# Counting edges with one-hot products: two columns of edges per product, one-hot values in runs of four

## The chip, the cores and the metric

The kernel runs on one core of one Trainium2 chip. The core has five engines that work side by side, each through its own queue: TensorE (PE: matrix products, and PEld: the loading of their weights), VectorE (DVE), ScalarE (ACT), GpSimd (POOL) and SyncE (SP, which starts transfers). The metric is the device time of one execution in microseconds (us), the median of several runs.

## The reference

The kernel is a four-layer network on 4608 tokens of 256 channels (two images of 48 x 48). The part that matters here is the graph attention inside layer 2. There are 1,048,576 edges, drawn for 65,536 nodes, while the graph has only T = 4608. An index that is too large reads the last node, and a target that is too large is dropped. So most of the valid edges have the last node as their source. Cut to what matters:

```python
M = Bc * Nc                                   # 4608 nodes
h = (x_flat @ W_gat).reshape(M, HEADS, NUM_EXPERTS)
e = leaky_relu(a_src[src] + a_dst[dst], negative_slope=0.2)
ee = jnp.exp(e - e_max[dst])
denom = jax.ops.segment_sum(ee, dst, num_segments=M)
msg = h[src] * (ee / (denom[dst] + 1e-16))[:, :, None]
agg = jax.ops.segment_sum(msg, dst, num_segments=M)
```

All edges from the last node to one target give the same term. The kernel therefore needs only a count for each of the 4608 targets, and treats the few other edges one by one.

## The kernel before

`Edges.sort_list` packs each edge into a key (a flag, the source counted down from the last node, 13 bits of target), and keeps the 64 largest keys of each of 16 lists in each of the 128 partitions: `slots`, 1024 keys a partition. In a key of the last node's edges the bits above the target hold the flag alone. `sort_rest` collects 16 columns of other keys into `oth` (16 x 4 = 64 columns are set aside), and the rest goes to DRAM.

`count_last` makes the count. The target is split into `lo` (its low 7 bits, 128 values) and `hi` (36 values). Of the 1024 columns of `slots` it takes 16 at a time, 64 groups in all. For each group VectorE writes two bf16 one-hot tiles: `ol` (L1322, 128 partitions x 16 columns x 128 values) and `oh` (L1326, 36 values x 16 columns). For each column TensorE multiplies them (L1328: `ol[:, j, :]` as weights, `oh[:, :, j]` as the moving operand of 36 columns), and all 1024 products add into one PSUM tile `cp`, 128 x 36. At the end one copy (L1333) moves `cp` to `cnt`. Both one-hot tiles have two buffers, so VectorE is at most two groups ahead of TensorE.

`count_last` is a generator that yields after each group. Its caller, `behind_gathers` in `graph_scores`, runs some steps of another piece of work after each: `pieces(AHEAD, BESIDE)`, the dense expert products for four stretches of 384 tokens. Each expert has seven steps of products (L1769, 192 moving columns, f32) with a VectorE or ScalarE operation behind each (L1778 to L1793, L1775, L1784), and 12 chains of second-layer products (L1810, 256 columns).

While this runs, GpSimd issues 128 indirect transfers (`gs`, L1427, and `gd`, L1431), one of each for each of 64 columns of other edges. They fetch rows of the node tables for `add_edges`. Later `add_edges` takes them in eight sets of eight columns (`GQ = 8`): a first sum `e<-gs,gd` (L1445) needs all 16 transfers of its set. Exponentials on ScalarE (L1448) follow, then for each column a one-hot row (`ol`, L1457), a wide product tile (`wide`, L1459, four buffers), and two products into `fp` (L1463, 360 columns). The sum at L1613 ends this stage, and the rest of the graph scores follow.

The order of the instructions in each engine's queue is not the order of the source. A scheduler sets it when the program is built, from its own estimates of durations, and each queue is then a fixed list. In the built program before, the first `e<-gs,gd` stands in VectorE's queue behind the last of the 64 groups.

Of the kernel before, what the change touches and what calls it, by code (L numbers as in the profile page):

```python
# [18 lines left out]
F32 = mybir.dt.float32  # L19
I32 = mybir.dt.int32  # L20
BF16 = mybir.dt.bfloat16
AF = mybir.ActivationFunctionType
ALU = mybir.AluOpType
# [4 lines left out]
P = 128  # L28
NB, C, HH, WW = 2, 256, 48, 48
L = HH * WW  # L30
T = NB * L
NT = T // P
# [66 lines left out]
def bc(ap, shape, axis):  # L99

    return ap.unsqueeze(axis).to_broadcast(shape)
# [1096 lines left out]
class Edges:  # L1198
# [93 lines left out]
    def count_last(self, E):  # L1292


        nc, tc = E.nc, E.tc
        n, LO = self.NL * self.SLOT, P
        GC = n // self.GROUPS
        HI = T // LO
        with (
            tc.tile_pool(name="gcnt", bufs=1) as wp,  # L1300
            tc.tile_pool(name="gcntps", bufs=1, space=PSUM) as ps,
        ):
            field = wp.tile([P, n], I32, name="field")
            ids_i = field[:, : HI * GC].rearrange("p (h g) -> p h g", h=HI)
            nc.gpsimd.iota(ids_i, pattern=[[1, HI], [0, GC]], base=0, channel_multiplier=0)
            ids = wp.tile([P, HI, GC], BF16, name="ids")
            nc.vector.tensor_copy(ids, ids_i)
            lo_ids = wp.tile([P, LO], BF16, name="lo_ids")
            nc.vector.tensor_copy(lo_ids, self.iota)
            bits = self.slots.bitcast(I32).rearrange("p l s -> p (l s)")  # L1310
            lo = wp.tile([P, n], BF16, name="lo")
            hi = wp.tile([P, n], BF16, name="hi")
            nc.vector.tensor_single_scalar(field, bits, LO - 1, ALU.bitwise_and)
            nc.vector.tensor_copy(lo, field)

            nc.vector.tensor_single_scalar(field, bits, 7, ALU.logical_shift_right)
            nc.vector.tensor_scalar(hi, field, float(-(self.FLAG >> 7)), None, ALU.add)
            cp = ps.tile([LO, HI], F32, name="cp")
            for g in range(n // GC):
                gs = slice(g * GC, (g + 1) * GC)  # L1320
                ol = wp.tile([P, GC, LO], BF16, tag="ol16", name="ol16", bufs=2)
                nc.vector.tensor_tensor(  # L1322
                    ol, bc(lo[:, gs], [P, GC, LO], 2), bc(lo_ids, [P, GC, LO], 1), ALU.is_equal
                )
                oh = wp.tile([P, HI, GC], BF16, tag="oh16", name="oh16", bufs=2)
                nc.vector.tensor_tensor(oh, bc(hi[:, gs], [P, HI, GC], 1), ids, ALU.is_equal)  # L1326
                for j in range(GC):
                    nc.tensor.matmul(  # L1328
                        cp, lhsT=ol[:, j, :], rhs=oh[:, :, j],
                        start=g == 0 and j == 0, stop=g == n // GC - 1 and j == GC - 1,  # L1330
                    )
                yield
            nc.vector.tensor_copy(self.cnt, cp)  # L1333


def target_maxima(E, edges, t_src, taken, best):
# [1502 lines left out]
```

## Time and profile before

| what | value |
|---|---|
| median of 3 runs (lowest to highest) | 4859.35 us (4858.32 to 4860.77) |
| profiled execution: its own time, its span | 4857.55 us, 4855.5 us |
| PE, DVE, ACT, POOL busy over the span | 4419.2, 3404.9, 2613.8, 2595.7 us |
| mean granted TensorE clock | 0.963 |
| the 64 groups: first `ol` to the copy of `cp` | 3373.05 to 3612.04 us |
| the 128 transfers: first start to last end | 3372.61 to 3639.77 us |
| products of `add_edges`: first start to the sum at L1613 | 3615.88 to 3695.88 us |

The profile is of one execution. Each row gives a start in us from the span's start and a length, with the engine, the line, and what was written from what. Rows that follow one another on an engine and are alike are merged, with their number (x16). What stands in brackets is the idle time of the engine before it and what ended it. TensorE's products overlap, so a length is a latency, and what a product costs in a stream is the distance between starts. An f32 product stands in the profile as two records.

### The profile page before, as it was taken

The page shows a single profiled execution, that of the slowest core. Times are in us where ns is not written, and L with a number is a line of the kernel's source. Part 1 is how long each engine was busy: PE and PEld are TensorE (multiplying, and loading weights), DVE is VectorE, ACT ScalarE, POOL GpSimd, SP SyncE. Part 2 cuts the span into 40 slices and gives each one's busy share as a digit, 9 for nine tenths or more (in the row PEclk, how much of TensorE's full clock was granted, in tenths as well). Part 3 has the DMA queues.
Part 4 walks back from the last instruction along what each step waited for, and adds up shares of the span by engine and source line. Part 5 has one row for each costly group of instructions (what it writes and reads, how often), then busy time and mean ns, then how long its engine had stood idle before and what let it go on. Part 6 is the DMA issues. An engine that isn't in the chain of part 4 may idle for free. (4 is left out here: it accounts for less than half of the span.)

```text
span 4855.5 us, 65017 instructions
## 1 busy us (share of the span) xinstructions
PE 4419.2 (91%) x23472; PEld 3283.1 (68%) x23472; DVE 3404.9 (70%) x5615; ACT 2613.8 (54%) x4390; POOL 2595.7 (53%) x2037
## 2 busy tenths in 40 slices
PE   7899999999999999988999999978998879999987
PEld 4666666667766667765555555547976558989855
DVE  4788888888888778887999924464887514453533
ACT  6888987888788888884223222323222423333311
POOL 3799887778888889887000000001880634445422
PEclk8999999999999999999999999999999889999988
DMA  3222222232221212223110000001111530000045
GB/s 98 71 87 86 79 92 80 87 99 90 76 83 56 73 63 82 86 75 124 47 39 31 33 5 13 1 35 34 33 27 55 159 106 24 14 11 7 11 142 161
DMA packets 160991, 312.47 MB, mean 64 GB/s; under 512 B 30855, under 2 KB 115055, under 8 KB 158084
## 3 DMA queue, kind: packets, MB, share of 16 engines
q1 hardware_dynamic: 144596, 271.49, 16.8%
q0 software_dynamic: 12304, 22.91, 2.1%
q10 hardware_dynamic: 3744, 13.66, 1.0%
q8 instruction: 192, 3.15, 0.3%
q14 instruction: 155, 1.27, 0.1%
HBM read 227.68 MB, written 80.31 MB: 63 GB/s over the span
## 5 line engine op out<-in xcount | busy, mean ns | idle before, releaser
L808 POOL TENSOR_TENSOR hcp<-ho,cc 128x768 f32<-128x768 f32 x768 | 1426.6, 1868 | 271.5 <-DVE ho L803 120.7
L672 PE MATMUL db<-ident,dbt 128*128 128x128 f32 x4608 | 791.1, 279 | 86.1 <-DVE ho L801 29.1
L672 PEld LDWEIGHTS db<-ident,dbt 128*128 128x128 f32 x4608 | 564.5, 142 | 408.9 <-issue 151.2
L698 PE MATMUL y<-ident,hcp 128*128 128x128 f32 x4608 | 742.7, 276 | 20.6 <-POOL hcp L808 20.5
L803 DVE TENSOR_TENSOR_SCAN ho<-he,state,db 128x384 f32<-128x384 f32 x640 | 627.6, 1005 | 123.2 <-PE db L672 85.7
L801 DVE TENSOR_TENSOR_SCAN ho<-he,state,db 128x384 f32<-128x384 f32 x640 | 622.6, 1002 | 121.6 <-PE db L672 95.2
L698 PEld LDWEIGHTS y<-ident,hcp 128*128 128x128 f32 x4608 | 557.8, 143 | 50.4 <-POOL hcp L808 26.9
L655 POOL TENSOR_SCALAR dbt<-dtt,bt 128x512 f32<-128x512 f32 x576 | 458.8, 806 | 118.1 <-ACT dtt L448 73.9
L662 ACT ACTIVATE he<-dt,negab 128x384 f32<-128x384 f32 x768 | 445.0, 609 | 128.1 <-DVE ho L803 124.7
L662 ACT ACTIVATE he<-dt,negaf 128x384 f32<-128x384 f32 x768 | 448.0, 611 | 107.4 <-DVE ho L801 100.5
L653 ACT ACTIVATE dbt<-dtt,bt 128x512 f32<-128x512 f32 x576 | 407.0, 712 | 4.3 <-PE db L672 3.9
L382 PE MATMUL mm<-xw,w_cv 128*128 128x384 f32 x768 | 316.1, 498 | 32.0 <-ACT xs L392 28.5
L1288 POOL PARTITION_ALL_REDUCE most<-most x1 | 0.4, 420 | 619.3 <-DVE most L1287 619.3
L1019 PE MATMUL pf<-t,wfc 128*128 128x384 f32 x768 | 254.9, 487 | 2.6 <-ACT hid L1023 2.2
L1038 PE MATMUL po<-hid,wfc 128*128 128x384 f32 x768 | 253.6, 486 | 0.0
L1023 ACT ACTIVATE hid<-pf,vec 128x384 f32<-128x384 f32 x192 | 109.7, 580 | 212.6 <-PE pf L1019 212.2
L1019 PEld LDWEIGHTS pf<-t,wfc 128*128 128x128 f32 x768 | 145.6, 190 | 106.0 <-ACT hid L1023 4.1
L1038 PEld LDWEIGHTS po<-hid,wfc 128*128 128x128 f32 x768 | 146.2, 190 | 101.5
L139 POOL TENSOR_TENSOR tv<-at 128x384 f32<-128x384 f32 x54 | 53.8, 997 | 253.1 <-ACT at L2507 121.0
L1810 PE MATMUL po<-w,hid 128*128 128x256 f32 x672 | 169.8, 382 | 0.0
L1191 POOL TENSOR_TENSOR xres<-xres,y 128x384 f32<-128x384 f32 x24 | 24.1, 1005 | 259.7 <-DVE y L1187 259.7
L382 PEld LDWEIGHTS mm<-xw,w_cv 128*128 128x128 f32 x768 | 118.9, 193 | 51.9 <-ACT xs L392 39.4
(659 smaller groups left out, 9115.5 us busy)
## 6 DMA issues: line engine op xcount, KB each, us to landing
cc<-bcd SPq DMA_DIRECT2D x96, 768.0 KB
xw<-xi_d SPq DMA_DIRECT2D x24, 774.0 KB
y_d<-y SPq DMA_DIRECT2D x28, 384.0 KB
down<-in_m_down SPq DMA_DIRECT2D x9, 1152.0 KB
up<-in_m_up SPq DMA_DIRECT2D x9, 1028.0 KB
xi_d<-xz SPq DMA_DIRECT2D x48, 192.0 KB
z_d<-xz SPq DMA_DIRECT2D x36, 256.0 KB
y<-z_d SPq DMA_DIRECT2D x12, 768.0 KB
```

The source lines that it names most:

```text
L382: nc.tensor.matmul(px, lhsT=w_cv[b, s][:, d * 4 + k, :], rhs=xw[:, d, o : o + W], start=k == 0, stop=k == 3,)
L653: nc.scalar.activation(to, at, AF.Copy, scale=b_n)
L655: nc.gpsimd.tensor_scalar(to, at, b_n, 1.0, ALU.mult, ALU.mult)
L662: nc.scalar.activation(hes[k], pc["dt"][:, d, :], AF.Exp, scale=nega[pc["s"]][:, d * NS + n : d * NS + n + 1])
L672: nc.tensor.transpose(dbs[k][:, j * P : (j + 1) * P], dbt[k // DB][:, j, d * P : (d + 1) * P], E.ident)
L698: nc.tensor.matmul(pc["yt"][j][:, d * P : (d + 1) * P], lhsT=hc[:, j * P : (j + 1) * P], rhs=E.ident, is_transpose=True, start=False, stop ...
L801: nc.vector.tensor_tensor_scan(to, he, db, init, ALU.mult, ALU.add)
L803: nc.vector.tensor_tensor_scan(to[:, ::-1], he[:, ::-1], db[:, ::-1], init, ALU.mult, ALU.add)
L808: nc.gpsimd.tensor_tensor(hc, ho, bc(cc, [P, 2, W], 1), ALU.mult)
L1019: nc.tensor.matmul(pf, lhsT=wfc1[:, k, f * P : (f + 1) * P], rhs=t1[:, k, :], start=k == 0, stop=k == 1,)
L1038: nc.tensor.matmul(po[m], lhsT=wfc2[:, f, m * P : (m + 1) * P], rhs=hid[:, i, :], start=f == 0, stop=f == 15,)
L1810: nc.tensor.matmul(po[:, j - a], lhsT=flat[:, f, j * P : (j + 1) * P], rhs=w2[:, e, f, :], start=f == 0, stop=f == FT - 1,)
```

## The change

The target is split at 6 bits in place of 7: `lo` has 64 values and `hi` has 72. VectorE writes both one-hot tiles with one helper. A group still has 16 columns of keys, laid out as 4 runs of 4: for each run, for each value, the four columns stand side by side. A product takes two columns of keys at once. Its weights are 2 x 64 one-hot values and its moving operand is 2 x 72, each element 4 places (8 bytes) from the next. There are 8 products a group in place of 16, and 512 in place of 1024. Their result is 128 x 144, of which two diagonal blocks of 64 x 72 are the counts. After the loop two copies take the blocks out (`own`), and two f32 products with a small matrix (`fold`) bring them into the old layout of `cnt`. `rows`, `fold`, `own` and `both` are new.

```diff
-        n, LO = self.NL * self.SLOT, P
+        n, LO, RUN = self.NL * self.SLOT, P // 2, 4
         GC = n // self.GROUPS
-        HI = T // LO
+        HI, NQ = T // LO, GC // RUN
...
-            ids_i = field[:, : HI * GC].rearrange("p (h g) -> p h g", h=HI)
-            nc.gpsimd.iota(ids_i, pattern=[[1, HI], [0, GC]], base=0, channel_multiplier=0)
-            ids = wp.tile([P, HI, GC], BF16, name="ids")
+            ids_i = field[:, : HI * RUN].rearrange("p (h g) -> p h g", h=HI)
+            nc.gpsimd.iota(ids_i, pattern=[[1, HI], [0, RUN]], base=0, channel_multiplier=0)
+            ids = wp.tile([P, HI, RUN], BF16, name="ids")
             nc.vector.tensor_copy(ids, ids_i)
-            lo_ids = wp.tile([P, LO], BF16, name="lo_ids")
-            nc.vector.tensor_copy(lo_ids, self.iota)
...
-            nc.vector.tensor_single_scalar(field, bits, 7, ALU.logical_shift_right)
-            nc.vector.tensor_scalar(hi, field, float(-(self.FLAG >> 7)), None, ALU.add)
-            cp = ps.tile([LO, HI], F32, name="cp")
+            nc.vector.tensor_single_scalar(field, bits, 6, ALU.logical_shift_right)
+            nc.vector.tensor_scalar(hi, field, float(-(self.FLAG >> 6)), None, ALU.add)
+            fold = wp.tile([P, 3, LO], F32, name="fold")
+            nc.vector.memset(fold, 0.0)
+            nc.vector.tensor_tensor(fold[:, 1], E.ident[:, :LO], E.ident[:, LO:], ALU.add)
+            cp = ps.tile([P, 2, HI], F32, tag="cp", name="cp")
             for g in range(n // GC):
                 gs = slice(g * GC, (g + 1) * GC)
-                ol = wp.tile([P, GC, LO], BF16, tag="ol16", name="ol16", bufs=2)
-                nc.vector.tensor_tensor(
-                    ol, bc(lo[:, gs], [P, GC, LO], 2), bc(lo_ids, [P, GC, LO], 1), ALU.is_equal
-                )
-                oh = wp.tile([P, HI, GC], BF16, tag="oh16", name="oh16", bufs=2)
-                nc.vector.tensor_tensor(oh, bc(hi[:, gs], [P, HI, GC], 1), ids, ALU.is_equal)
-                for j in range(GC):
-                    nc.tensor.matmul(
-                        cp, lhsT=ol[:, j, :], rhs=oh[:, :, j],
-                        start=g == 0 and j == 0, stop=g == n // GC - 1 and j == GC - 1,
+
+                def rows(src, m, name):
+                    t = wp.tile([P, NQ, m, RUN], BF16, tag=name, name=name, bufs=2)
+                    nc.vector.tensor_tensor(
+                        t, bc(src[:, gs].rearrange("p (q r) -> p q r", r=RUN), [P, NQ, m, RUN], 2),
+                        bc(ids[:, :m], [P, NQ, m, RUN], 1), ALU.is_equal,
                     )
+                    return t
+
+                ol, oh = rows(lo, LO, "ol16"), rows(hi, HI, "oh16")
+                for q in range(0, NQ, 2):
+                    for r in range(RUN):
+                        nc.tensor.matmul(
+                            cp, lhsT=ol[:, q : q + 2, :, r], rhs=oh[:, q : q + 2, :, r],
+                            start=g == 0 and q == 0 and r == 0,
+                            stop=g == n // GC - 1 and q == NQ - 2 and r == RUN - 1,
+                        )
                 yield
-            nc.vector.tensor_copy(self.cnt, cp)
+            own = wp.tile([P, 2, NT], F32, name="own")
+            for z in range(2):
+                ps_ = slice(z * LO, (z + 1) * LO)
+                nc.vector.tensor_copy(own[ps_], cp[ps_, z].rearrange("p (h r) -> p r h", r=2))
+            both = ps.tile([P, NT], F32, tag="cp", name="both")
+            for z in range(2):
+                nc.tensor.matmul(
+                    both, lhsT=fold[:, 1 - z : 3 - z].rearrange("p a l -> p (a l)"), rhs=own[:, z],
+                    start=z == 0, stop=z == 1,
+                )
+            nc.vector.tensor_copy(self.cnt, both)
```

More of the change, by code (lines that the diff above doesn't have):

```diff
@@ L1325, in count_last @@
-                oh = wp.tile([P, HI, GC], BF16, tag="oh16", name="oh16", bufs=2)
-                nc.vector.tensor_tensor(oh, bc(hi[:, gs], [P, HI, GC], 1), ids, ALU.is_equal)
-                for j in range(GC):
-                    nc.tensor.matmul(
-                        cp, lhsT=ol[:, j, :], rhs=oh[:, :, j],
-                        start=g == 0 and j == 0, stop=g == n // GC - 1 and j == GC - 1,
-                    )
-                yield
-            nc.vector.tensor_copy(self.cnt, cp)
+                def rows(src, m, name):
[5 more added lines that the diff above has]
+                    return t
@@ new lines, in count_last @@
+                ol, oh = rows(lo, LO, "ol16"), rows(hi, HI, "oh16")
[6 more added lines that the diff above has]
+                        )
+                yield
+            own = wp.tile([P, 2, NT], F32, name="own")
```

## The prediction

> **What bounds the kernel now.** I read the page first, for the engine that fills the span.
>
> ```profile
> PE 4419.2 (91%) x23472; PEld 3283.1 (68%) x23472; DVE 3404.9 (70%) x5615; ACT 2613.8 (54%) x4390; POOL 2595.7 (53%) x2037
> ```
>
> TensorE leads, but this is a mean over stages. So the second view is the table by windows around the change (columns: window, length, then busy us of PE, PEld, DVE, ACT and POOL with their counts, granted clock, DMA share, GB/s).
>
> ```profile
> 3373.00:3612.00 239.00, 229.65 (x1840) 212.56 (x1840) 207.00 (x222) 62.98 (x144) 205.18 (x112) 0.96 0.16 31
> 3612.00:3696.00 84.00, 80.13 (x257) 50.12 (x257) 78.20 (x177) 1.83 (x8) 22.89 (x17) 0.94 0.05 2
> ```
>
> The 64 groups of the count fill the first window. TensorE is busy for 229.65 of 239 us there, VectorE for 207 and GpSimd for 205. All three are close to full, so what helps one may only uncover the next. Third, the groups of instructions in that window (count, then busy us and mean ns):
>
> ```profile
> L1322 DVE TENSOR_TENSOR ol<-lo,lo_ids 128x2048 bf16<-128x2048 bf16 x64 | 146.2, 2284 | 2.2 <-PE cp L1328 2.2
> L1431 POOL DMA_INDIRECT gd<-t_dst,didx x56 | 105.2, 1878 | 17.1 <-issue 17.1
> L1810 PE MATMUL po<-w,hid 128*128 128x256 f32 x384 | 95.3, 382 | 0.0
> L1328 PE MATMUL cp<-oh,ol 128*128 128x36 bf16 x1024 | 79.5, 246 | 10.4 <-DVE oh L1326 10.4
> L1326 DVE TENSOR_TENSOR oh<-hi,ids 128x576 bf16<-128x576 bf16 x64 | 29.0, 453 | 0.0
> ```
>
> Fourth, the timeline of some groups in the middle, which shows distances on TensorE and the hold on GpSimd:
>
> ```profile
> 3450.32 1.89 PE L1810 MATMUL po<-w,hid 128*128 128x256 f32 x8
> 3453.82 0.81 PE L1769 MATMUL sy<-xn,w 128*128 128x192 f32 x4
> 3455.85 0.94 POOL L1431 DMA_INDIRECT gd<-t_dst,didx  x1 [0.30 <-issue]
> 3459.27 2.28 DVE L1322 TENSOR_TENSOR ol<-lo,lo_ids 128x2048 bf16<-128x2048 bf16 x1
> 3459.64 2.73 POOL L1431 DMA_INDIRECT gd<-t_dst,didx  x1 [0.30 <-issue]
> 3459.72 1.25 PE L1328 MATMUL cp<-oh,ol 128*128 128x36 bf16 x16
> 3461.47 0.45 DVE L1326 TENSOR_TENSOR oh<-hi,ids 128x576 bf16<-128x576 bf16 x1
> ```
>
> A stream's distance is (length of the merged row - one product) / (number - 1). It is (1.25 - 0.246) / 15 = 0.067 us for a product of the count, (1.89 - 0.382) / 7 = 0.215 for a record of 256 columns, and (0.81 - 0.327) / 3 = 0.161 for one of 192. An issue of a transfer takes 0.94 + 0.30 us when nothing holds it. One that meets an `ol` and `oh` back to back takes 2.73. Last, the view of the tile `gs`, for who waits for these transfers:
>
> ```profile
> L1445 DVE TENSOR_TENSOR e<-gs,gd x8: 181/187/194, 3611.0 to 3656.7; 128x32 f32<-128x32 f32 x8
> DMA to landing us min/median/max: 2.3/3.6/6.2
> ```
>
> The first of these sums runs at 3611.0, when all groups are written. Nobody waits for a transfer today.
>
> **VectorE's part.** `oh` shows that bf16 with runs of 16 goes at two elements a cycle: 576 elements in 453 ns. `ol`, whose one input repeats a single element, goes at one: 2048 in 2284. From the two, an element costs 0.52 or 1.04 ns over about 0.15 us. The new tiles have 1024 and 1152 elements in runs of 4. At the faster rate they cost 0.68 and 0.75 us, 1.43 a group in place of 2.74; at the slower 1.22 and 1.35. I take the faster, since `oh` is the row with adjacent elements on every operand. VectorE sheds 64 x 1.31 = 84 us.
>
> **TensorE's part.** The count costs 1024 x 0.067 = 68.6 us now. Afterwards it is 512 products of 144 columns. Lower bound of one: 0.067, today's pair with the same 128 weights. Upper bound: if today's pace is set by the 36 moving columns that stand 32 bytes apart, 0.067 / 36 x 144 = 0.27. The nearest contiguous row is the f32 transpose at L698, 128 columns with 128 weights, at 0.109. I take 0.088, halfway from 0.067 to 0.109, since columns 8 bytes apart are much nearer to contiguous than 32 bytes. That is 45 us, a saving of 23.
>
> [...]
>
> **What is late next: the transfers.** In the built changed program VectorE's queue holds the first `e<-gs,gd` behind group 8, the second behind 9, the third behind 12 and the fourth behind 14 of 64. Before, the first stood behind group 64. Each waits for its 16 transfers, and behind it wait all later `ol` and `oh`, and the copies (L1778 to L1793) that the expert products need. So TensorE starves as well. GpSimd starts at 3372.61 as before, since what stands ahead of it changes little (a smaller iota and cast, a small memset and add: nothing).
>
> The fourth sum needs 64 transfers. Free of holds they take 64 x 1.245 = 79.7 us. With today's holds they would take 64 x (3639.77 - 3372.61) / 128 = 133.6. Today's extra is 0.84 us x about 115 transfers in the loop = 97 us, under 64 x 2.74 = 175 us of holds, or 0.55 us for each us of hold. Until the fourth sum the new program has 14 pairs of 1.31 (the two less their overlap) and four `wide` of 0.9, 22 us, so 12 us extra. The 64th issue ends at 3372.6 + 79.7 + 12 = 3464.3. It started 0.94 earlier and lands 3.6 after that: 3467. Bounds: 3455 without holds, 3509 with today's.
>
> Without the waits VectorE would be there by 14 x 3 us, about 3415. Some 50 us of stall thus stand against 23 us of savings and today's slack of 10.
>
> [...] No run yet shows VectorE held at such a sum. [...] If VectorE could pass over the wait, the change would give the gain of the first rival.
>
> **The sum.** After the fourth sum there remain on TensorE, counted in the built order, 168 products of 192 columns and 155 of 256, two records each: 336 x 0.161 + 310 x 0.215 = 120.8 us. To this come 50 groups x 8 x 0.088 = 35.2. The first pair must be written before TensorE goes on (1.3), and a restart at a lower clock costs something: the granted clock was 0.62 in 3600 to 3620, where TensorE also waited, against 1.00 before it. I take 1.7, between 0 and 20 x 0.38 = 7.6. VectorE needs about 1.3 + 0.7 a group there, TensorE 3.1: TensorE binds. The loop ends at 3467 + 1.3 + 120.8 + 35.2 + 1.7 = 3626, against 3612: 14 us later.
>
> Behind the loop, `add_edges` is bound by TensorE:
>
> ```profile
> 3615.88 24.31 PE L1463 MATMUL fp<-wide,ol 128*128 128x360 f32 x70 [3.87 <-DVE wide L1459]
> ```
>
> The 3.87 us of waiting go, since four `wide` are ready by then. The copies of `own` and the two small products cost about 0.5 on this path, the rest hides behind those four. That gives 3.4 back. Elsewhere the queues change by a few places only.
>
> Total: 14 - 3.4 = +10.6 us. The profiled execution took 4857.55 and becomes 4868; its span is 2.05 us less. The median of the runs is 1.8 above it, so 4870.
>
> **The rivals.** *The transfers don't hold VectorE* (faster): the loop is then TensorE's work, 212 products of 192 and 191 of 256 columns (68.3 + 82.1) + 45 us + today's 10 us of gaps = 205, ending near 3579: 33 us earlier, and 3.4 more behind it: 4823. It decides if 64 transfers land within the first 42 us, 0.66 us each. No row is below 0.94. 5%. A milder form, no hold on GpSimd and 0.067 us a product, ends at 4850: 5%.
>
> *The strided operands bind TensorE* (slower): at 0.15 to 0.27 us a product the 50 groups cost 25 to 73 us more: 4895 to 4943. For it speaks that the count's 36 columns take as long as they do; against it that steps shrink from 32 to 8 bytes. The weights, contiguous today, may pay as well. 15%.
>
> *Runs of four don't give the faster rate*: pairs of 2.4 us, as now. VectorE then needs 3.1 us a group, level with TensorE, and the holds make the fourth sum 9 us later: about 4879. 7%.
>
> My forecast, the stall with 0.067 to 0.11 us a product, has the other 68%, and its own range is 4855 to 4890.
>
> **How the numbers follow.** A measurement of this kernel tells about 0.2%, 9.7 us, from no change. The forecast stands at +10.6, and two fifths of it fall within 9.7; with the milder form's edge this makes 0.32 for the same. Faster by more: 0.09, the first rival and half of the milder one and of the forecast's lowest edge. Slower: 0.59. The range leaves out the first rival and the worst strides: 4851 to 4902.
>
> **What would show it.** Right: a row `e<-gs,gd` with VectorE idle ahead of it for 10 us or more, three times between 3400 and 3470, released by transfers; low TensorE shares there; transfers nearer to 1.4 us than to 2.1; `ol` near 0.68 us; products about 0.09 us apart; `fp` starting right behind `cp`. Wrong: those sums start without idle time, or the products stand 0.15 us apart or more.

## The result and the profile after

The changed kernel takes 4881.97 us in the median of 5 runs (4878.72 to 4890.37), the kernel before 4859.35 beside it: a ratio of 1.0049 [1.0038, 1.0061], 22.6 us slower. The profiled execution took 4881.97 us with a span of 4879.9, 24.4 more than before's span. The prediction was 4870 (4851 to 4902), slower at 0.59.

Engine shares of the page after:

```profile
PE 4417.7 (91%) x22964; PEld 3274.8 (67%) x22964; DVE 3328.2 (68%) x5618; ACT 2617.9 (54%) x4394; POOL 2499.2 (51%) x2037
```

VectorE is 77 us less busy and GpSimd 97 us, TensorE hardly (4417.7 after 4419.2), although the count has half as many products. The program is slower with less work on every engine that was full in the loop, so the loss should be waiting. The windows, cut at the fourth sum and at the end of the loop (columns as in the prediction):

```profile
3369.80:3457.00 87.20, 47.21 (x240) 41.09 (x240) 32.31 (x70) 16.13 (x31) 67.09 (x66) 0.77 0.12 15
3457.00:3643.20 186.20, 183.81 (x1079) 164.69 (x1080) 104.25 (x178) 50.03 (x117) 65.83 (x63) 0.98 0.16 31
3643.20:3721.50 78.30, 78.30 (x264) 49.53 (x263) 71.48 (x152) 3.03 (x8) 0.00 (x0) 1.00 0.02 6
```

In the first 87 us TensorE works 47 and VectorE 32; only GpSimd, with 66 transfers, is at work throughout. From the fourth sum to the end of the loop TensorE is nearly full (184 of 186 us). The loop grew from 239.0 to 273.4 us. The timeline of the sums (in brackets VectorE's idle time ahead of each, and what ended it):

```profile
3394.18 0.19 DVE L1462 TENSOR_TENSOR e<-gs,gd 128x32 f32<-128x32 f32 x1 [7.69 <-DMA gd<-t_dst,didx]
3415.03 0.20 DVE L1462 TENSOR_TENSOR e<-gs,gd 128x32 f32<-128x32 f32 x1 [17.37 <-DMA gd<-t_dst,didx]
3436.16 0.19 DVE L1462 TENSOR_TENSOR e<-gs,gd 128x32 f32<-128x32 f32 x1 [10.32 <-DMA gd<-t_dst,didx]
3456.58 0.22 DVE L1462 TENSOR_TENSOR e<-gs,gd 128x32 f32<-128x32 f32 x1 [14.79 <-DMA gd<-t_dst,didx]
```

The four waits add up to 50.2 us. The sums stand 21 us apart, the time of 16 transfers at 1.02 + 0.30 us. That TensorE starves with VectorE shows behind the fourth sum: it waits for `u`, which VectorE writes only after the sum.

```profile
3458.78 0.55 DVE L1804 COPY u<-sx 128x384 f32<-128x384 f32 x1
3459.39 1.65 PE L1786 MATMUL sx<-tx,w 128*128 128x192 f32 x4 [12.22 <-DVE u L1804]
```

At the sum VectorE has written 14 groups and TensorE has multiplied 13 of them, 104 of the 512 products. The groups of the same stretch, and one group's row of the timeline:

```profile
L1334 PE MATMUL cp<-oh,ol 128*128 128x144 bf16 x512 | 78.9, 309 | 3.0 <-DVE oh L1325 3.0
L1444 POOL DMA_INDIRECT gs<-t_src,sidx x64 | 67.9, 1062 | 23.9 <-issue 19.2 <-DVE didx L1416 4.7
L1325 DVE TENSOR_TENSOR oh<-hi,ids 128x1152 bf16<-128x1152 bf16 x64 | 48.2, 752 | 0.0
L1325 DVE TENSOR_TENSOR ol<-lo,ids 128x1024 bf16<-128x1024 bf16 x64 | 44.1, 690 | 53.3 <-PE cp L1334 53.1
```
```profile
3561.78 1.22 PE L1334 MATMUL cp<-oh,ol 128*128 128x144 bf16 x8
```

`ol` and `oh` take 0.69 and 0.75 us, as predicted. The products stand (1.22 - 0.309) / 7 = 0.130 us apart. So 512 of them cost 67 us, and 1024 at 0.067 cost 69: on TensorE the change saves nothing. VectorE now waits 53 us for TensorE ahead of `ol`; its savings lie idle there.

### The profile page after: what moved, and what is told of

Read it like the earlier page. It is cut to its first block, busy times and chain, and to the rows that moved or that the text cites. A ratio compares the mean times of both kernels' runs of the same rounds, so it can differ in the third digit from the quotient of the medians.

```text
span 4879.9 us, 64022 instructions
## 1 busy us (share of the span) xinstructions
PE 4417.7 (91%) x22964; PEld 3274.8 (67%) x22964; DVE 3328.2 (68%) x5618; ACT 2617.9 (54%) x4394; POOL 2499.2 (51%) x2037
## 5 line engine op out<-in xcount | busy, mean ns | idle before, releaser
L139 POOL TENSOR_TENSOR tv<-at 128x384 f32<-128x384 f32 x54 | 53.8, 997 | 253.4 <-ACT at L2524 121.2
```

## Experiments

Two questions were open: how much of the loss the places of the sums are, and what makes a product 0.13 us. Each kernel is a small edit of the changed kernel or of the kernel before. Each ratio is to the kernel before, run beside it; that kernel's median moved between 4854.5 and 4859.9 us, so kernels run at different times are compared by their ratios. "Late" below means this edit (cut to its main lines), which puts the sums behind the last group in VectorE's queue:

```diff
+                if g == n // GC - 1:
+                    nc.vector.tensor_scalar(self.gate, oh[:, 0, 0, 0:1], 0.0, None, ALU.mult)
...
-        nc.vector.tensor_tensor(e, gs[:, :, 0:H], gd[:, :, 0:H], ALU.add)
+        if gate is None:
+            nc.vector.tensor_tensor(e, gs[:, :, 0:H], gd[:, :, 0:H], ALU.add)
+        else:
+            nc.vector.scalar_tensor_tensor(e, gs[:, :, 0:H], gate, gd[:, :, 0:H], ALU.add, ALU.add)
```

**late_run4: the sums late, nothing else.**

> The changed kernel, with the sums e<-gs,gd kept behind the last group of the count (a [128,1] tile made of the last group's one-hot values, times 0, is added to each sum). Theory 1 (the waits of VectorE at these sums are the main loss): no idle time ahead of the first sum, and all 64 groups run at the pace that the changed kernel shows behind its fourth sum, 186.6 / 50 = 3.73 us a group. That makes a loop of 239 us in place of 273.4, so 4882 - 34 = 4848 us (4840 to 4856). Theory 2 (the loss lies in the products, and the waits are covered by slack): less than 10 us come back, 4872 us or more. Distance of the products under both 0.13 us.

Measured: 4833.63 us, ratio to before 0.9956 [0.9943, 0.997]. VectorE's timeline at the first sums, and the windows of the loop:

```profile
3593.03 0.15 DVE L1341 TENSOR_SCALAR gate<-oh 128x1 f32<-128x1 bf16 x1
3593.44 0.25 DVE L1468 SCALAR_TENSOR_TENSOR e<-gs,gate,gd 128x32 f32<-128x32 f32 x1 [0.26 <-DVE gate L1341]
```
```profile
3373.50:3414.10 40.60, 40.12 (x241) 35.93 (x240) 28.51 (x54) 10.67 (x25) 31.77 (x30) 0.96 0.12 26
3414.10:3595.50 181.40, 181.40 (x1081) 162.53 (x1081) 103.07 (x180) 51.37 (x119) 102.86 (x99) 1.00 0.18 33
```

The wait for transfers is gone, and 45 us (by the ratios) to 48 us (by the medians) come back: theory 1. The first `ol` starts at 3372.07, 1.4 us ahead of the first window. So the first 241 products and pieces take 42.0 us where the changed kernel took 87.2 for its first 240, and the others take 181.4 against 186.2: 45 of the 50 us that the loop loses lie ahead of the fourth sum. Behind the loop the late sums cost 2.7 us (80.5 in place of 77.7 to the sum that ends the stage).

The expected 4848 was 14 us too high. It scaled a pace per group, 186.6 / 50, and this pace was too slow in three ways: it held the restart behind the fourth sum (some 5 us); TensorE had 51 groups to do there, not 50; and the groups ahead of it have fewer pieces of the experts beside them, 241 - 104 = 137 of some 810 records, 17%, for 13 of 64 groups, 20%.

**before_early: the old count, and four sums in the new places.** The edit (cut) writes each of the first four sums behind its group:

```diff
             for i, _ in enumerate(edges.count_last(E)):
+                if i + 1 in (8, 9, 12, 14):
+                    first_sum((8, 9, 12, 14).index(i + 1))
```

> The kernel before with its old count, but the first four sums e<-gs,gd written behind groups 8, 9, 12 and 14, where the changed program has them. If these places are what costs: VectorE is idle ahead of them, 40 to 80 us in all (the pairs of 2.74 us hold the transfers, so longer than in the changed kernel), 4890 to 4930 us. If the old count's slack covers them: below 4870 us.

Measured: 4906.78 us, ratio 1.0101 [1.0087, 1.0115], 47 us slower. VectorE's groups in the window 3370 to 3480:

```profile
L1441 DVE TENSOR_TENSOR e<-gs,gd 128x32 f32<-128x32 f32 x4 | 0.9, 222 | 51.7 <-DMA gd<-t_dst,didx 51.7
```

The places alone cost the old kernel as much as the changed one (its loop takes 288.3 us in place of 239.0), and its slack covers next to nothing.

**early_run2: the changed kernel with RUN = 2.**

> The changed kernel with runs of two and nothing else changed: the four sums keep their places behind groups 8, 9, 12 and 14. If the waits at these sums are set by the transfers alone, VectorE is idle about 50 us ahead of them as with runs of four, the 400 products behind the fourth sum save 400 x 0.066 = 26 us, and the kernel comes to 4882 - 26 = 4856 us (4848 to 4862), 50 us above late_run2. If the waits are set by TensorE's pace, they shrink with it: 4835 us or less.

```diff
-        n, LO, RUN = self.NL * self.SLOT, P // 2, 4
+        n, LO, RUN = self.NL * self.SLOT, P // 2, 2
```

Measured: 4861.13 us, ratio 1.0001 [0.9993, 1.001]. VectorE is idle 53.8 us ahead of the four sums (50.2 in the changed kernel). A faster product doesn't shorten the waits: the transfers set them. Against the late kernel with the same runs (next) it is 1.05% slower by the ratios, some 50 us, as expected.

**late_run2, late_run8, late_run1: the step of TensorE's columns.** In late_run4 the same line is changed, to 2, 8 and 1.

> As late_run4, with runs of two (columns 4 bytes apart for TensorE). Theory 1 with the step of 8 bytes as what makes a product 0.131 us: the products come to about 0.09 us, 512 x 0.04 = 20 us less on TensorE, 4828 us, if VectorE keeps its 0.69 and 0.75 us. Theory 3 (not the step but 144 columns with two columns of edges make it 0.131): products stay at 0.13 us, 4848 us. Where VectorE falls to the slower rate, ol and oh cost 1.2 and 1.35 us, which shows in their rows.

> As late_run4, with runs of eight (columns 16 bytes apart). Theory 1 with the step as cause: products of 0.18 us or more, at least 512 x 0.05 = 25 us more on TensorE, 4873 us or more. Theory 3: 0.13 us, 4848 us. VectorE's rows the same as in late_run4.

> As late_run4, with runs of one, so that the 128 weights and the 144 moving columns are contiguous. Theory 1 with the step as cause: products of 0.06 to 0.07 us, 512 x 0.065 = 33 us less on TensorE, ol and oh at the slower rate of 1.2 and 1.35 us, 4815 to 4830 us if TensorE still binds, up to 4840 where VectorE (about 3.3 us a group) does. GpSimd's transfers are held again (mean 1.4 us or more), but nobody waits for them before the loop ends. Theory 3: 0.13 us, 4848 us or more.

Measured: 4803.62 us (0.9897 [0.9882, 0.9912]), 4900.69 (1.0098 [1.0084, 1.0112]) and 4818.08 (0.9926 [0.9912, 0.9939]). Timeline rows of the count, in the order of runs of two, eight and one:

```profile
3472.72 0.68 PE L1335 MATMUL cp<-oh,ol 128*128 128x144 bf16 x8
```
```profile
3471.76 1.74 PE L1335 MATMUL cp<-oh,ol 128*128 128x144 bf16 x6
```
```profile
3473.95 0.66 PE L1335 MATMUL cp<-oh,ol 128*128 128x144 bf16 x8
```

One product alone takes 0.228, 0.438 and 0.231 us in these kernels, so the distances are (0.68 - 0.228) / 7 = 0.065, (1.74 - 0.438) / 5 = 0.260 and (0.66 - 0.231) / 7 = 0.061 us. From 2 to 4 bytes the step costs next to nothing (0.061 and 0.065 us); from there to 16 bytes the distance doubles with it (0.130 at 8, 0.260 at 16). Theory 3 falls. (Late_run2 is 24 us below the 4828 that was expected, since 0.09 us had been taken for a product at 4 bytes.) Of these three, VectorE's rate drops only with runs of one (`ol` takes 0.688 us with runs of two, 0.691 with runs of eight):

```profile
L1326 DVE TENSOR_TENSOR oh<-hi,ids 128x1152 bf16<-128x1152 bf16 x64 | 86.2, 1347 | 0.0
L1326 DVE TENSOR_TENSOR ol<-lo,ids 128x1024 bf16<-128x1024 bf16 x64 | 77.8, 1215 | 2.0 <-PE cp L1335 1.9
```

There VectorE hardly waits for TensorE any more (1.9 us, 35.5 with runs of two) and binds: it is busy for 197 of the loop's 201 us. Runs of two have both rates: 0.688 and 0.751 us for `ol` and `oh`.

**w8_m4 and w4_m8: whose step.** Late kernels in which only one of the two operands stands in runs of four:

```diff
-                ol, oh = rows(lo, LO, "ol16"), rows(hi, HI, "oh16")
+                ol, oh = rows(lo, LO, "ol16", 4), rows(hi, HI, "oh16", 2)
```

That is w8_m4, cut to the line that matters (the last argument is the length of a run); w4_m8 has 2 and 4 there.

> As late_run4, but only the weights (ol) stand in runs of four, 8 bytes apart; the moving columns (oh) stand in runs of two, 4 bytes apart. Theory W (the step of the weights sets the distance of the products): 0.131 us, near 4834 us. Theory M (the step of the moving columns does): 0.065 us, near 4804 us.

> The other way round: weights in runs of two (4 bytes apart), moving columns in runs of four (8 bytes apart). Theory W: 0.065 us, near 4804 us. Theory M: 0.131 us, near 4834 us. For W speaks that the kernel before had moving columns 32 bytes apart at 0.067 us a product of 36: in proportion to late_run8 (0.261 us for 144 columns at 16 bytes) these would cost 0.13.

Measured: 4803.91 us (0.9889 [0.9875, 0.9904]) and 4838.62 (0.9951 [0.9936, 0.9966]). The rows, first with the weights 8 bytes apart, then with the moving columns:

```profile
3470.71 0.70 PE L1335 MATMUL cp<-oh,ol 128*128 128x144 bf16 x8
```
```profile
3469.90 1.21 PE L1337 MATMUL cp<-oh,ol 128*128 128x144 bf16 x8
```

Distances of 0.067 and 0.129 us: theory M. The step of the weights costs nothing here; that of the moving columns is the whole difference. My argument for W, the old product, then needs another explanation.

**w4_m32: moving columns 32 bytes apart, as in the kernel before.** The two numbers are 2 and 16.

> As w4_m8, with the moving columns in runs of sixteen, 32 bytes apart as in the kernel before; weights 4 bytes apart. If the cost of a moving column goes on in proportion to its step (0.065 us a product at 4 bytes, 0.131 at 8, 0.261 at 16): 0.52 us, about 4803 + 512 x 0.455 = 5036 us. If it stops growing at 16 bytes: 0.26 us, about 4803 + 512 x 0.196 = 4903 us. The second would mean that the 0.067 us of the old product were 36 columns at that pace (36 / 144 x 0.261 = 0.065), and not its 128 weights.

Measured: 4912.26 us, ratio 1.0119 [1.0099, 1.014], from two runs.

```profile
3471.98 2.25 PE L1338 MATMUL cp<-oh,ol 128*128 128x144 bf16 x8
```

(2.25 - 0.439) / 7 = 0.259 us, as against 0.260 at 16 bytes: from 16 to 32 the cost doesn't grow. That is 1.80 ns a column, and the old product's 36 columns come to 0.065 us at that rate, which is the 0.067 that it took. (The time is 9 us above what was expected. `ol` is slower here, 1.09 us, but VectorE waits 106 us for TensorE, so that is not it. In the profiles, late_run8, with products as long, is 10 us shorter: 3 of these lie in the loop, the others in stages ahead of and behind what was changed. Their cause stays open.)

**one_run2: late_run2 with one column of edges a product.** There is no fold.

```diff
-        n, LO, RUN = self.NL * self.SLOT, P // 2, 2
+        n, LO, RUN = self.NL * self.SLOT, P, 2
...
-                            cp, lhsT=ol[:, q : q + 2, :, r], rhs=oh[:, q : q + 2, :, r],
+                            cp, lhsT=ol[:, q, :, r], rhs=oh[:, q, :, r],
```

> late_run2 with one column of edges a product: 128 and 36 one-hot values, 1024 products, weights and moving columns 4 bytes apart, no fold at the end. [...] If neither binds at 36 columns (0.03 us or less), as fast as late_run2. VectorE: ol about 1.2 us, oh 0.45.

Measured: 4800.95 us, ratio 0.9898 [0.9881, 0.9914]; late_run2 had 0.9897.

```profile
L1332 PE MATMUL cp<-oh,ol 128*128 128x36 bf16 x1024 | 37.1, 180 | 4.2 <-DVE oh L1323 4.2
```
```profile
3500.51 0.56 PE L1332 MATMUL cp<-oh,ol 128*128 128x36 bf16 x16
```

(0.56 - 0.180) / 15 = 0.025 us a product, with 128 weights each. So 128 new weights keep no product longer than that, and 1024 such products cost 26 us where 512 wide ones cost 33. What sets the 0.025 no run here shows. Two columns of edges per product are worth nothing; the layout is what counts.

**before_m4: the kernel before with that one step changed.**

```diff
-                oh = wp.tile([P, HI, GC], BF16, tag="oh16", name="oh16", bufs=2)
+                oh = wp.tile([P, GC // 2, HI, 2], BF16, tag="oh16", name="oh16", bufs=2)
...
-                        cp, lhsT=ol[:, j, :], rhs=oh[:, :, j],
+                        cp, lhsT=ol[:, j, :], rhs=oh[:, j // 2, :, j % 2],
```

> The kernel before with one edit: its oh16 in runs of two, so that the 36 moving columns of a product are 4 bytes apart and not 32. Weights, one column of edges a product, sizes and the places of the sums (behind group 64) as before. If the step of the moving columns made the old 0.067 us, a product takes 0.025 as in one_run2, and TensorE sheds 1024 x 0.042 = 43 us of the loop; VectorE, with 207 us of work there, then binds: a loop of about 212 us in place of 239, 4857 - 27 = 4830 us (4822 to 4840). If it needs the weights' new layout too: 0.067 us, 4857 us.

Measured: 4844.43 us, ratio 0.9971 [0.996, 0.9981], above the expected 4822 to 4840. A group's products, windows of the loop and of the products behind it, and the last sum:

```profile
3470.89 0.56 PE L1331 MATMUL cp<-oh,ol 128*128 128x36 bf16 x16
```
```profile
3382.50:3586.30 203.80, 188.90 (x1836) 171.19 (x1835) 201.20 (x216) 62.47 (x144) 177.07 (x88) 0.96 0.15 35
3586.30:3690.50 104.20, 83.91 (x260) 51.84 (x260) 78.39 (x179) 1.83 (x8) 50.67 (x39) 0.88 0.10 3
```
```profile
3650.93 0.19 DVE L1448 TENSOR_TENSOR e<-gs,gd 128x32 f32<-128x32 f32 x1 [11.88 <-DMA gd<-t_dst,didx]
```

The products come to (0.56 - 0.180) / 15 = 0.025 us. The first `ol` starts at 3379.66, 2.8 us ahead of the first window, so the loop shrinks from 239.0 to 206.7 us, more than expected, with VectorE (201.20 of 203.80 in the window) as its bound. But 19 of those 32 us are given back: the stretch behind takes 103.3 us in place of 83.8, because GpSimd, held by the long `ol` as before (2.28 us, with a mean of 1.80 us a transfer; late_run4, whose `ol` takes 0.69, has 1.06), still has 39 transfers to do when the loop ends, and the last two sums wait 8.1 and 11.9 us for them. I had taken it that nobody would wait. VectorE's faster layout is thus worth something after all: one_run2, which has runs of two in `ol` as well, and late sums, takes 1.14 us a transfer, has none left when its loop ends, and is 0.7% faster.

**The version that beats both** is late_run2, or one_run2 with less code: about 1.0% below before, and some 1.5% below the changed kernel (0.9897 / 1.0049). The stretch behind its loop shows that the transfers are done in time:

```profile
3561.00:3642.00 81.00, 81.00 (x281) 52.02 (x280) 75.68 (x167) 2.36 (x9) 0.00 (x0) 1.00 0.02 5
```

## Why the prediction was right, and where its terms were off

**What is late next: right.** The sums hold VectorE at the four places and TensorE starves behind it; 50.2 us of idle time against "some 50 us of stall". Keeping the sums late gives 45 to 48 us back, and putting them into the old kernel costs 47. VectorE passed over none of these waits: the four rows show it idle for 7.7, 17.4, 10.3 and 14.8 us.

**The fourth sum: 7 to 8 us too late.** It came 86.7 us after the first `ol` (at 3369.85), where the prediction had 94. The hold on GpSimd was oversized: up to the fourth sum a transfer took 1.02 us (67.09 for 66) against 0.94 unheld. The 64th issue ended 84.9 us after the first began (3370.11 to 3455.03) where 79.7 + 12 had been taken, and the transfers landed after 2.7 us (median) in place of 3.6. The rule of 0.55 us per us of hold, taken from pairs of 2.74 us, does not carry over: 22 us of hold cost 5.2, or 0.24 for each.

**The loop behind the fourth sum: 186.6 us in place of 159.** This is the term that was mis-sized. The product was taken as 0.088 us and measured 0.130, and there were 408 of them left, not 400: 408 x 0.130 = 53.0 us in place of 35.2, 17.8 more. The choice "columns 8 bytes apart are much nearer to contiguous than 32 bytes" was the mistake. In these runs the rate has steps: 4 bytes (0.065 us) are nearly as good as contiguous (0.061), 8 bytes cost twice that (0.130), 16 and 32 four times (0.260 and 0.259). The second piece is the backlog: 1079 - 408 = 671 records of pieces were left, not the 646 counted from the queues, since TensorE lagged behind the place of the fourth sum; 25 records at 0.187 us are 4.7 us. Late_run4 does this stretch in 181.4 us, at a granted clock of 1.00 and without idle time, so the restart cost 5.2 (186.6 less 181.4) where 1.3 + 1.7 was taken: 2.2 more. The last 2.9 us are in late_run4 too: its 181.4 us are that much more than the 178.5 that 408 products and 671 pieces come to at these distances. No run here says where they belong.

**The saving of 23 us on TensorE: wrong.** It was 2 us (1024 x 0.067 less 512 x 0.130). The old 0.067 was read as the price of a pair with 128 weights, and so as a lower bound; it was the price of 36 columns 32 bytes apart. The prediction had this reading as its upper bound, 0.27, and for 32 bytes it was right (0.259 in w4_m32). What failed was the guess of how the cost falls between 32 bytes and contiguous.

The lower bound of 0.067 for 144 columns didn't hold either: the runs show 0.061 and 0.065 us at steps of 2 and 4 bytes.

**Behind the loop: right in kind.** `fp` starts at 3643.4, right behind `cp`. The stretch takes 77.7 us in place of 83.9, 6.2 less where 3.4 was predicted.

**VectorE: right.** Both tiles run at the faster rate, `ol` in 0.690 us and `oh` in 0.752, and the savings end as idle time. The 128 elements between the two cost 62 ns here and 132 with runs of one (late_run1): 0.48 and 1.03 ns an element, where 0.52 and 1.04 were taken.

**The sum.** The loop ended 20.4 us later than predicted, counted from its start (273.4 against 253), and the stretch behind gave 2.8 more back; the stages ahead of the loop ran 3.2 us shorter in this execution, and the rest stayed within 0.6. So +10.6 became +24.4 in the span. The direction came from the stall, which was read rightly. That the time fell inside the range owes something to luck: the fourth sum came 7 us earlier and the loop behind it took 28 longer than predicted, and the two partly cancel.

Of the rivals, "the strided operands bind TensorE" held in its mechanism: at 0.13 its edge of 0.15 us was just missed, and the moving operand was the one to blame, not the weights. The forecast's stall was the larger part all the same.

## What to carry to other kernels

When an engine gets faster, look in its built queue for what moves up: an instruction that waits for transfers, placed early by the schedule, can cost more than the change saves, and a cheap dependence that keeps it late gave most of it back here (45 to 48 us of some 50). Before cutting the number of small products, find out what sets their distance: here it was neither the weights nor the count but the step of the moving columns, and keeping that at 4 bytes (runs of two bf16: 0.065 us a product in place of 0.130) was worth more than halving the count. And ask of each hold that seems harmless who would wait if the stretch before it shrank; before_m4 gave back more than half of its gain that way.

## What the runs showed of the hardware

- In these kernels the distance of the count's bf16 products went by the step between moving columns: for 144 columns 0.061 us at 2 bytes (late_run1), 0.065 at 4 (late_run2), 0.130 at 8 (the changed kernel), 0.260 at 16 (late_run8), 0.259 at 32 (w4_m32). The step of the weights made no difference: 0.065 us with 4 bytes (late_run2) and 0.067 with 8 (w8_m4), both with moving columns 4 bytes apart.
- Products of 36 columns, 4 bytes apart, with new 128 weights each followed one another at 0.025 us (one_run2, before_m4).
- VectorE's comparison kept its faster rate down to runs of two bf16 (0.688 us for 1024 elements, late_run2) and lost it at runs of one (1.215 us, late_run1). In w4_m32, where the pairs of one input stand 32 bytes apart, runs of two took 1.092 us; with pairs 8 bytes apart (w4_m8) they took 0.692.
